# Two-layer image network on one core: x with positions on partitions for the selective scan, projections and LayerNorm moved between images

## The chip, the cores and the metric

The kernel runs on one core of a Trainium2 chip. The metric is the device time of one execution in microseconds. Five engines work in parallel, each through its own instruction queue in order: PE (TensorE), DVE (VectorE), ACT (ScalarE), POOL (GpSimd) and SP (SyncE, which here only issues DMAs).

## The reference

Eight images of 56 x 56 pixels with 192 channels pass two residual layers. Layer 0 (group norm, three gated projections to 576 channels, Toeplitz products along rows and columns) is not touched by the change. Layer 1 is a state-space block on 384 inner channels with 16 states:

```python
xz = gn(x) @ W_in.T
xc, z = split(xz)                       # 384 and 384 channels
xc = silu(depthwise_conv3x3(xc) + conv_b)
# eight orders of the 3136 pixels: rows and columns, there and back, every other line turned round
for k in range(8):
    dt, B, C = split(x_proj_weight[k] @ xs[k])      # 12, 16 and 16 rows
    delta = softplus(dt_projs_weight[k] @ dt + bias)
    h = exp(delta * A) * h + (delta * xs[k]) * B    # step by step along the order
    y[k] = sum_n(h * C) + D * xs[k]
y = layernorm(sum_k(y[k] back in pixel order))
out = x + (y * silu(z)) @ W_out.T
```

## The kernel before

After layer 0 for all images (lines 113 to 370) and a preparation of image 0 (lines 415 to 485), each image has a **scan stage** (488 to 892) and a **LayerNorm stage** (895 to 1217). The LayerNorm stage of image b also prepares image b + 1.

*Scan stage.* The 3136 steps of each of the eight orders are cut into chunks of W = 63, so there are 400 chunks, and three blocks of 128 channels for each: 1200 units per image. A unit is one `tensor_tensor_scan` on DVE over 16 states of 64 elements (`scan`, L740). It reads `da` = exp(delta * A) from ACT (`exps`, L704: 16 instructions for four chunks of one channel block) and `bx` from PSUM (`products`, L725: the products of delta * x with B for all states, as matmuls with a block-diagonal image of B). Before the scan ACT copies the last state of the chunk before into `bx` (`before`, L736). After it POOL multiplies h by the broadcast C (`times_c`, L751), PE turns and sums that over the states into `yps` (`sums`, L848), ACT copies it out (L875), and SP stores y with positions as rows (L760).

What a unit needs is made for a group of up to eight chunks (`Group`), in this order: SP loads x with channels on partitions in the order of the scan (`xs`, L542); PE projects it to the rows of steps, B and C (`project`, L549), ACT copies them out, mirrored where the order runs backwards (`projected`, L562); C goes to DRAM and comes back broadcast over partitions (`to_dram`, `broadcast`, L566 and L573); B is written element by element into a zeroed DRAM image along its diagonal and read back (`diagonal_out`, `diagonal_in`, L650 and L658; ten such images, zeroed once at L395); PE and ACT make delta (`steps`, L580, L589, and one softplus for the group, L593). Then for each pair of chunks POOL multiplies delta by x (`product`, L616), PE turns the product so that positions lie on partitions (`turn`, L625), ACT copies it to `dut` (`turned`, L633), and SP makes a second copy with the halves swapped (`swapped`, L641).

A hand-written table (`plan`) gives every step of a group its place relative to the group's first unit f, and a loop over units writes the order on every engine:

```python
s = f - 11 + 6 * p
at("POOL", s - 1, self.product, p)
at("PE", s, self.turn, p)
at("ACT", s + 1, self.turned, p)
```

The scheduler does not reorder (`tc.manual_schedule()`). `px`, `pd` and `pt` share one PSUM bank (`pmisc`, one buffer). Four `da` buffers are in turn.

*LayerNorm stage.* Seven tiles of eight image rows (448 pixels). For each, four loads of `yk` bring the eight y's of 112 pixels (16 DMAs each, three buffers), and PE turns and adds them into `ysum` (96 transposes a tile, L1092). DVE adds D * x (L1111); mean and variance come from matmuls with a matrix of 1/384 (L1123, L1146); the rest is on DVE and ACT with channels on partitions. Beside it, for the next image: projection (L949), convolution as nine matmuls with diagonal weights for each of three channel blocks (L967), and copies of the result in three orders on DVE and POOL (L991, L993, L1010, L1012), stored as `xo`. This stage has a hand-written order too.

Of the kernel before, what the change touches and what calls it, by code (L numbers as in the profile page):

```python
# [70 lines left out]
SC = 4  # L71
SIZES = (8, 8, 8, 8, 8, 8, 2)
# [16 lines left out]
def conv_kernel(ctx: ExitStack, tc: tile.TileContext, a: dict, out: bass.AP):  # L89
# [18 lines left out]
    gstat = const.tile([CP, B, 2, 2], F32, name="gstat")  # L108

# [274 lines left out]

    xod = [[dram.tile([128, NB, L], F32, name=f"xo{b}_{o}") for o in range(3)] for b in range(B)]
    ytd = [dram.tile([K, L, DI], F32, name=f"yt{b}") for b in range(B)]

    bdd = [dram.tile([2, 64 * 64 * N], F32, name=f"bd{i}") for i in range(NI)]  # L390
    with tc.tile_pool(name="none", bufs=1) as p:
        none = p.tile([128, 64 * N], F32, name="none")
        nc.vector.memset(none, 0.0)
        for t in bdd:
            nc.sync.dma_start(t.rearrange("h (s x) -> (h s) x", s=64), none)  # L395

    def halves(t):

        return t.rearrange("p d (h w) -> p d h w", w=HW)

    for b in range(B):

        def normed(pool, t):

            x1 = pool.tile([CP, 2, T], F32, name="x1")
            nc.sync.dma_start(x1, x1d[b][:, :, t * T : (t + 1) * T])
            xn = pool.tile([CP, 2, T], F32, name="x1n")
            for c in range(2):
                nc.vector.tensor_scalar(
                    xn[:, c], x1[:, c], gstat[:, b, c, 0:1], gstat[:, b, c, 1:2], ALU.subtract, ALU.mult  # L410
                )
            return x1, xn


        if b == 0:
            with ExitStack() as st:
                one = st.enter_context(tc.tile_pool(name="prep1", bufs=1))
                pre = st.enter_context(tc.tile_pool(name="prep", bufs=2))
                pm = st.enter_context(tc.tile_pool(name="pp", bufs=4, space=PSUM))
                win = one.tile([CP, 2, 2 * DI], F32, name="win")  # L420
                nc.sync.dma_start(win, a["W_inT"])
                xp = [one.tile([128, HW + 2, HW + 2], F32, name=f"xp{d}") for d in range(NB)]
                dg = one.tile([128, NB, 9, 128], F32, name="dg")
                for d in range(NB):
                    for edge in (xp[d][:, 0, :], xp[d][:, HW + 1, :], xp[d][:, :, 0], xp[d][:, :, HW + 1]):
                        nc.gpsimd.memset(edge, 0.0)  # L426
                    for j in range(9):
                        nc.vector.tensor_scalar(
                            dg[:, d, j, :], ident, cw[:, d, j : j + 1], None, ALU.mult
                        )  # L430
                for t in range(NT):
                    _, xn = normed(pre, t)
                    for d in range(NB):
                        pp = pm.tile([128, T], F32, name="pp")
                        for c in range(2):
                            nc.tensor.matmul(
                                pp, win[:, c, d * 128 : (d + 1) * 128], xn[:, c], start=(c == 0), stop=(c == 1)
                            )
                        nc.scalar.copy(
                            xp[d][:, 1 + t * RT : 1 + (t + 1) * RT, 1 : HW + 1],  # L440
                            pp.rearrange("p (h w) -> p h w", w=HW),
                        )
                xc = one.tile([128, NB, L], F32, name="xc")
                xcv = xc.rearrange("p d (h w) -> p d h w", w=HW)
                for t in range(NT):
                    for d in range(NB):
                        pc = pm.tile([128, RT, HW], F32, name="pc", tag="pp")
                        for j in range(9):
                            dy, dx = divmod(j, 3)
                            nc.tensor.matmul(  # L450
                                pc,
                                dg[:, d, j, :],
                                xp[d][:, t * RT + dy : t * RT + dy + RT, dx : dx + HW],
                                start=(j == 0),
                                stop=(j == 8),
                            )
                        nc.scalar.activation(
                            xc[:, d, t * T : (t + 1) * T],
                            pc.rearrange("p h w -> p (h w)"),
                            AF.Silu,  # L460
                            bias=cb[:, d : d + 1],
                        )
                    for o in range(2):
                        xo = pre.tile([128, NB, T], F32, name=f"xo{o}")
                        for par in range(2):
                            src = xcv[:, :, t * RT + par : (t + 1) * RT : 2, :]
                            dst = halves(xo)[:, :, par::2, :]
                            if par != o:
                                src = src[:, :, :, ::-1]
                            if o:  # L470
                                nc.gpsimd.tensor_copy(dst, src)
                            else:
                                nc.vector.tensor_copy(dst, src)
                        nc.sync.dma_start(xod[b][o][:, :, t * T : (t + 1) * T], xo)
                xct = xcv.rearrange("p d h w -> p d w h")
                for t in range(NT):
                    xo = pre.tile([128, NB, T], F32, name="xo2", tag="xo0")
                    for par in range(2):
                        src = xct[:, :, t * RT + par : (t + 1) * RT : 2, :]
                        dst = halves(xo)[:, :, par::2, :]  # L480
                        if par:
                            nc.gpsimd.tensor_copy(dst, src[:, :, :, ::-1])
                        else:
                            nc.vector.tensor_copy(dst, src)
                    nc.sync.dma_start(xod[b][2][:, :, t * T : (t + 1) * T], xo)


        with ExitStack() as st:
# [11 lines left out]
            das = [one.tile([128, SC, N, W + 1], F32, name=f"da{i}") for i in range(4)]  # L500
            for t in das:
                nc.gpsimd.memset(t[:, :, :, 0], 0.0)
            dus = [one.tile([128, NB, 2, W + 1], F32, name=f"du{i}") for i in range(2)]
            for t in dus:
                nc.gpsimd.memset(t[:, :, :, W], 0.0)
# [6 lines left out]
            class Group:  # L512


                def __init__(self, k, c0, nch, i):
# [7 lines left out]
                    self.bufs = 1 if self.small else 2  # L523
                    u0 = c0 * W
                    self.m = min(self.n, L - u0)
                    self.p0 = L - u0 - self.m if self.rev else u0
                    self.cb, self.dut, self.bd = [], [], []

                def load(self):
                    if self.c0 == 0:  # L530
                        xpw = pre.tile([128, NB, XR], F32, name="xpw")
                        nc.sync.dma_start(xpw, a["x_proj"][:, :, self.k, :])
                        dtw = pre.tile([R + 1, DI], F32, name="dtw")
                        nc.sync.dma_start(dtw, a["dt_w"][:, self.k, :])
                        weights[self.k] = xpw, dtw
                    n, m = self.n, self.m
                    self.xs = pre.tile([128, NB, n], F32, name="xs", tag="xs" + self.tag, bufs=self.bufs)
                    lo = n - m if self.rev else 0
                    if m < n:
                        z = slice(0, n - m) if self.rev else slice(m, n)  # L540
                        nc.gpsimd.memset(self.xs[:, :, z], 0.0)
                    nc.sync.dma_start(  # L542
                        self.xs[:, :, lo : lo + m], xod[b][self.o][:, :, self.p0 : self.p0 + m]
                    )

                def project(self, d):
                    if d == 0:
                        self.px = pmisc.tile([XR, 512], F32, name="px", tag="misc")
                    nc.tensor.matmul(  # L549
                        self.px[:, : self.n],  # L550
                        weights[self.k][0][:, d],
                        self.xs[:, d],
                        start=(d == 0),
                        stop=(d == NB - 1),
                    )

                def projected(self):
                    self.pxs = pre.tile([XR, self.n], F32, name="pxs", tag="pxs" + self.tag, bufs=self.bufs)
                    src = self.px[:, : self.n]
                    if self.rev:  # L560
                        src = src[:, ::-1]
# [333 lines left out]
        with ExitStack() as st:  # L895
# [293 lines left out]
            for t in range(NT):  # L1189
# [14 lines left out]
                if Z:  # L1204
                    Z.project()
# [86 lines left out]
```

## Time and profile before

| | us |
|---|---|
| median of 3 runs | 30519.63 |
| lowest and highest | 30509.42, 30534.07 |
| profiled execution | 30517.28 |
| its span | 30515.5 |
| PE, DVE, ACT, POOL busy | 28382.8, 23796.3, 22305.0, 22200.9 |
| first scan of image 0, of image 1 | 3671.3, 7055.4 |
| last scan of image 0, of image 7 | 6554.3, 30241.6 |

The profiled execution takes 1.8 us more than its span, which is what lies around it. Busy time is that of one engine; engines work at the same time, so these don't add up. In lines of the costliest groups stand line, engine, operation, output <- inputs with partitions x elements, the count, then busy us, mean ns of one, and the idle time in front with what ended it. A fp32 matmul has two records. Back-to-back instructions of DVE overlap a little: a scan is recorded with 2.26 us, and starts follow each other by 2.177 us at best.

### The profile page before, as it was taken

To read this page: it belongs to the slowest core of one execution; us is meant where nothing else is said; L and a number is where in the kernel's file an instruction comes from. 1 tells how busy PE (TensorE), PEld (TensorE's weight loads), DVE (VectorE), ACT (ScalarE), POOL (GpSimd) and SP (SyncE) were. 2 spreads that over 40 slices of the span, in tenths; PEclk is the share of its full clock that TensorE was granted. 3 is DMA by queue.
4 is the path that set the end of the run, shared out by engine and by line. 5 is a ranking of instruction groups with operands and counts; after the bars stand their busy time and mean duration, and the time that the engine had idled before them with its cause. 6 is when DMAs were issued, how large, how long until landed. Compare 5 with 4: busy or idle time off the path is not lost.

```text
span 30515.5 us, 475124 instructions
## 1 busy us (share of the span) xinstructions
PE 28382.8 (93%) x156976; PEld 16133.2 (53%) x156976; DVE 23796.3 (78%) x13460; ACT 22305.0 (73%) x58955; POOL 22200.9 (73%) x11592
## 2 busy tenths in 40 slices
PE   7999899988999899989999899989999899989998
PEld 5555455554555455554555455545555455545555
DVE  3444399967999499958998599949997699949997
ACT  2233388857898488848898488849887588848886
POOL 0000299957999399948998499939997599939996
PEclk9999999999999899999999999999999999989999
DMA  3222355555555555555555555545555555545555
GB/s 80 64 59 59 81 150 151 149 149 143 151 151 149 140 151 151 149 144 147 151 150 148 143 149 150 152 139 151 152 150 149 143 149 151 151 140 151 149 151 157
DMA packets 5635967, 4229.72 MB, mean 139 GB/s; under 512 B 3712112, under 2 KB 5007920, under 8 KB 5625968
## 3 DMA queue, kind: packets, MB, share of 16 engines
q1 hardware_dynamic: 5600368, 4192.09, 52.5%
q8 instruction: 1265, 20.73, 0.3%
q10 hardware_dynamic: 33152, 7.23, 0.2%
q14 instruction: 1182, 9.68, 0.1%
HBM read 3389.38 MB, written 508.43 MB: 128 GB/s over the span
## 4 chain that ended last, share of the span: by engine, by line
PE 49%; ACT 9%; POOL 5%; DMA 5%; issue 4%; DVE 3%; SPq 2%; ACTq 0%; POOLq 0%; DVEq 0%
PE bx L725 18%; PE yps L848 17%; ACT da L704 5%; POOL hc L751 5%; PE px L549 3%; PE pc L967 3%; PE pd L580 2%; DVE h L740 2%; DMA cbt<-cd 2%; PE pt L625 1%; DMA yt<-yt 1%; PE ysum L1092 1%; ACT L704 1%; ACT L593 1%; PE pp L949 1%
## 5 line engine op out<-in xcount | busy, mean ns | idle before, releaser
L740 DVE TENSOR_TENSOR_SCAN h<-da,bx 128x1024 f32<-128x1024 f32 x9600 | 21374.7, 2273 | 2122.0 <-ACT bx L736 1862.3
L751 POOL TENSOR_TENSOR hc<-h,cbt 128x1008 f32<-128x1008 f32 x9600 | 20552.9, 2167 | 1289.0 <-PE yps L848 584.9
L704 ACT ACTIVATE da<-delta,A_logs 128x252 f32<-128x252 f32 (+1 forms) x39936 | 17030.9, 489 | 76.7 <-DVE h L740 66.2
L725 PE MATMUL bx<-bd,dus 63*128 63x504 f32 x19200 | 10468.4, 633 | 223.2 <-DVE h L740 219.8
L725 PE MATMUL bx<-bd,dut 63*128 63x504 f32 x19200 | 10453.4, 633 | 224.3 <-DVE h L740 222.4
L848 PEld LDWEIGHTS yps<-ident,hc 128*126 128x126 f32 x76800 | 8360.9, 141 | 4045.8 <-issue 2361.8
L848 PE MATMUL yps<-ident,hc 128*126 128x128 f32 x76800 | 9500.1, 277 | 458.4 <-ACT yt L875 423.8
L725 PEld LDWEIGHTS bx<-bd,dut 63*128 63x128 f32 x19200 | 2901.9, 186 | 2616.4 <-DVE h L740 1531.0
L725 PEld LDWEIGHTS bx<-bd,dus 63*128 63x128 f32 x19200 | 2903.3, 186 | 1085.1 <-issue 664.0
L736 ACT COPY bx<-h 128x16 f32<-128x16 f32 x9408 | 1655.5, 176 | 1658.1 <-PE bx L725 1606.4
L426 POOL MEMSET xp<- 128x58 f32 x12 | 1.3, 193 | 3402.0 <-DMA x<-x1d 3401.9
L991 POOL COPY xo<-xp 128x672 f32<-128x672 f32 x98 | 70.5, 749 | 2852.9 <-ACT xp L974 2852.9
L616 POOL TENSOR_TENSOR du<-delta,xs 128x378 f32<-128x378 f32 x1600 | 1588.2, 993 | 174.9 <-ACT delta L593 173.6
L549 PE MATMUL px<-xs,xpw 128*64 128x504 f32 (+1 forms) x2688 | 1237.3, 571 | 215.5 <-DMA xs<-xo 215.5
L875 ACT COPY yt<-yps 126x256 f32<-126x256 f32 x2400 | 862.8, 360 | 719.1 <-PE yps L848 708.3
L580 PE MATMUL pd<-pxs,dtw 13*128 13x504 f32 x2304 | 1299.4, 644 | 68.2 <-ACT dut L633 29.3
L625 PEld LDWEIGHTS pt<-ident,du 128*128 128x128 f32 x4800 | 498.8, 141 | 1252.8 <-issue 565.6
L974 ACT ACTIVATE xp<-pc,conv_b 128x448 f32<-128x448 f32 x147 | 93.4, 636 | 1346.5 <-PE pc L967 1346.4
L967 PE MATMUL pc<-xp,dg 128*128 128x448 f32 x2646 | 1019.6, 538 | 0.0
L1111 DVE SCALAR_TENSOR_TENSOR y<-xc,dsum,ysum 128x224 f32<-128x224 f32 x336 | 125.4, 442 | 1133.6 <-PE ysum L1092 1133.6
L625 PE MATMUL pt<-ident,du 128*128 128x128 f32 x4800 | 880.6, 293 | 45.3 <-POOL du L616 38.4
L549 PEld LDWEIGHTS px<-xs,xpw 128*64 128x64 f32 x2688 | 298.6, 138 | 1116.0 <-issue 873.9
(137 smaller groups left out, 16721.2 us busy)
## 6 DMA issues: line engine op xcount, KB each, us to landing
cbt<-cd SPq DMA_DIRECT2D x1600, 1008.0 KB
bd<-bd SPq DMA_DIRECT2D x3200, 256.0 KB
dus<-dut SPq DMA_DIRECT2D x3200, 96.0 KB
yk<-yt SPq DMA_DIRECT2D x3584, 84.0 KB
yt<-yt SPq DMA_DIRECT2D x9408, 31.5 KB
xs<-xo SPq DMA_DIRECT2D x384, 756.0 KB
xo<-xo SPq DMA_DIRECT2D x168, 672.0 KB
bd<-pxs SPq DMA_DIRECT2D x3200, 3.9 KB
```

Source lines behind the costliest of these rows:

```text
L549: nc.tensor.matmul(self.px[:, : self.n], weights[self.k][0][:, d], self.xs[:, d], start=(d == 0), stop=(d == NB - 1),)
L580: nc.tensor.matmul(self.pd[:, : self.n], weights[self.k][1][:, d * 128 : (d + 1) * 128], self.pxs[0 : R + 1], start=True, stop=True,)
L616: nc.gpsimd.tensor_mul(self.du[:, :, :, :W], self.delta[:, :, part].rearrange("p d (c t) -> p d c t", t=W), xs[:, :, part].rearrange("p d ...
L625: nc.tensor.transpose(self.pt[:, d * 128 : (d + 1) * 128], self.du[:, d].rearrange("p c t -> p (c t)"), ident,)
L704: yield nc.scalar.activation(da[:, : self.nc, n, 1:], src.rearrange("p (c t) -> p c t", t=W), AF.Exp, scale=an[:, G.k, self.d, n : n + 1],)
L725: nc.tensor.matmul(self.bx[:, r, :, 1:], G.dut[p][q ^ r][rows, self.d * 128 : (self.d + 1) * 128], G.bd[p][rows, q, :, :W], start=True, st ...
L736: nc.scalar.copy(self.bx.rearrange("p r n t -> p (r n) t")[:, :, 0], src)
L740: nc.vector.tensor_tensor_scan(self.h.rearrange("p n t -> p (n t)"), das[self.P.buf][:, self.slot].rearrange("p n t -> p (n t)"), self.bx. ...
L751: nc.gpsimd.tensor_tensor(hc, self.h[:, :, 1:], self.G.cb[self.c // 2][:, :, q * W : (q + 1) * W], ALU.mult)
L848: nc.tensor.matmul(yps[:, t // 4 % 2, t // 2 % 2], lhsT=hcs[t // 2][:, n].rearrange("p c t -> p (c t)"), rhs=ident, start=(n == 0), stop=( ...
L875: nc.scalar.copy(y, yps[:, s // 4 % 2])
L967: nc.tensor.matmul(pc, dg[:, d, j, :], xp[:, d, t * RT + dy : t * RT + dy + RT, dx : dx + HW], start=(j == 0), stop=(j == 8),)
```

## The change

*x for the scan.* x is stored in DRAM with one pixel's 384 channels as a row (`xtd`), in three orders. A pair of chunks is loaded with positions on partitions (`inputs`, four buffers `xts`). delta alone is turned by PE, and DVE multiplies the turned delta in PSUM by x into `dut`. POOL's `product`, ACT's `turned` and the loads of `xs` are gone. For orders that run backwards nothing is mirrored ahead: delta is kept in pixel order, and the exponentials, the product with C and the places of stores are read backwards instead.

*Projections.* The rows of steps, B and C for all eight orders are made in the stage between images, with two directions of one order in one matmul of 128 rows (`rows`), and stored in `pxd` by DMAs of ACT's queue. The scan stage loads steps (`dt`), C (`cd`) and B's diagonals from `pxd`. There are twenty zeroed images for the diagonals (backward orders have their own), written ahead of layer 0's weights instead of after layer 0.

*Stage between images.* One class for preparation and LayerNorm, run for b = -1 to 7, in an order found by the scheduler instead of written by hand. y is stored with the directions of one order side by side, so a load of four rows has two DMAs of 3072-byte rows and four of 6144-byte rows (`load_y`, six buffers). POOL and DVE add the eight y's and D * x with positions on partitions; mean and variance of a pixel come from `bn_stats`; the scaling is one ACT instruction for 112 pixels, and only then PE turns the sum (12 transposes a tile). The convolution of channel blocks 0 and 2 runs on DVE, that of block 1 on PE. PE turns the convolved x (12 transposes a tile), and SP stores it in the orders; the mirrored lines of two orders are copied from DRAM to DRAM (`mirror`).

*Scan stage, smaller edits.* Five `da` buffers (`NR`); the softplus of a small group in three instructions; other places of the first large group's steps.

The core of the diff:

```diff
 class Group:
     def load(self):
-        self.xs = pre.tile([128, NB, n], F32, name="xs", ...)
-        nc.sync.dma_start(self.xs[...], xod[b][self.o][:, :, self.p0 : self.p0 + m])
+        self.dt = pre.tile([R + 1, self.n], F32, name="dt", tag="dt" + self.tag, bufs=1)
+        nc.sync.dma_start(*self.part(self.dt, 0, R + 1, 0, self.m, self.n))
+        self.cd = cdp.tile([GC // 2, N, 2 * W], F32, name="cd")
+        for p in range(self.npr):
+            nc.sync.dma_start(*self.part(self.cd[p], 48, N, p * 2 * W, e, 2 * W))
-    def project(self, d): ...
-    def projected(self): ...
-    def to_dram(self): ...
+    def inputs(self, p):
+        xt = self.xt[p] = xts[(self.i // 2 + p) % 4]
+        nc.sync.dma_start(xt, lines_of(xtd[b][self.o], at, (W, 2), (1, W + 1)))
+        ...
-    def product(self, p):
-        nc.gpsimd.tensor_mul(self.du[:, :, :, :W], self.delta[...], xs[...])
     def turn(self, p):
         nc.tensor.transpose(
             self.pt[:, d * 128 : (d + 1) * 128],
-            self.du[:, d].rearrange("p c t -> p (c t)"),
+            self.delta[:, d, first : first + 2].rearrange("p c t -> p (c t)"),
             ident)
-    def turned(self, p):
-        nc.scalar.copy(dut, self.pt[:, :DI])
+    def product(self, p):
+        nc.vector.tensor_mul(dut, self.pt[:, :DI], self.xt[p])
     def diagonal_out(self, p):
-        nc.sync.dma_start(to, self.pxs[32 : 32 + N, u : u + W]...)
+        nc.sync.dma_start(to, pxd[b][self.place, 32 : 32 + N][:, u : u + e]...)
     def plan(self, at):
-        at("POOL", s - 1, self.product, p)
+        at("SP", x if soon and p == 0 else s - 6, self.inputs, p)
         at("PE", s, self.turn, p)
-        at("ACT", s + 1, self.turned, p)
+        at("DVE", s + 1, self.product, p)
 ...
 class Unit:
     def times_c(self, hc):
+        if self.G.rev:
+            q, h = 1 - q, h[:, :, ::-1]
         nc.gpsimd.tensor_tensor(hc, h, self.G.cb[...], ALU.mult)
 ...
 class Next:      # the next image
     def conv(self):
+        for j in range(9):
+            for d in range(NB):
+                if d == 1:
+                    nc.tensor.matmul(acc, dg[:, j], src, start=(j == 0), stop=(j == 8))
+                elif j:
+                    nc.vector.scalar_tensor_tensor(acc, src, w, acc, ALU.mult, ALU.add)
+                else:
+                    nc.vector.tensor_scalar(acc, src, w, None, ALU.mult)
+    def rows(self, g):
+        nc.tensor.matmul(ps, pxw[:, d, g], x[:, t * RT : (t + 1) * RT], ...)
+        nc.scalar.activation(dst, src, AF.Identity, bias=pxb)       # twice, every other line
+        nc.scalar.dma_start(to[:, t * T : (t + 1) * T], px)
 ...
 class Tile:      # LayerNorm of this image
+    def pairs(self, i):
+        nc.gpsimd.tensor_tensor(xt, xt, dsb, ALU.mult)
+        nc.gpsimd.tensor_tensor(yk[:, 0:4], yk[:, 0:4], yc, ALU.add)
+    def total(self, i):
+        nc.vector.tensor_add(yk[:, 0:2], yk[:, 0:2], yk[:, 2:4])
+        nc.vector.tensor_add(yk[:, 0], yk[:, 0], yk[:, 1])
+        nc.vector.tensor_add(ys, yk[:, 0], xt)
+        nc.vector.bn_stats(self.st[:, i], ys)
+        nc.vector.bn_aggr(self.mv[:, i], self.st[:, i : i + 1])
-    def centre(self): ...
-    def scale(self): ...
```

## The prediction

> **What bounds the kernel now.** I read the busy table first, then the costliest groups, then stretches of the span, then the chain of waits.
>
> ```profile
> PE 28382.8 (93%) x156976; PEld 16133.2 (53%) x156976; DVE 23796.3 (78%) x13460; ACT 22305.0 (73%) x58955; POOL 22200.9 (73%) x11592
> ...
> L740 DVE TENSOR_TENSOR_SCAN h<-da,bx 128x1024 f32<-128x1024 f32 x9600 | 21374.7, 2273 | 2122.0 <-ACT bx L736 1862.3
> L751 POOL TENSOR_TENSOR hc<-h,cbt 128x1008 f32<-128x1008 f32 x9600 | 20552.9, 2167 | 1289.0 <-PE yps L848 584.9
> ...
> L616 POOL TENSOR_TENSOR du<-delta,xs 128x378 f32<-128x378 f32 x1600 | 1588.2, 993 | 174.9 <-ACT delta L593 173.6
> L549 PE MATMUL px<-xs,xpw 128*64 128x504 f32 (+1 forms) x2688 | 1237.3, 571 | 215.5 <-DMA xs<-xo 215.5
> ```
>
> All four engines are near full, so shares alone decide nothing. The busy time by stretch (start and end, length; PE, PEld, DVE, ACT, POOL; granted clock; DMA share; GB/s) separates the stages:
>
> ```profile
> 3405.00:3671.00 266.00, 202.04 (x505) 95.60 (x505) 33.41 (x62) 41.23 (x71) 24.71 (x43) 0.84 0.31 95
> 3671.00:6557.00 2886.00, 2772.20 (x15613) 1555.95 (x15613) 2671.98 (x1202) 2580.05 (x7031) 2746.97 (x1405) 0.99 0.58 149
> 6557.00:7055.00 498.00, 386.99 (x1445) 217.22 (x1445) 129.41 (x209) 82.73 (x121) 26.55 (x44) 0.86 0.49 142
> ...
> 30244.00:30515.00 271.00, 198.75 (x943) 126.33 (x941) 96.45 (x148) 42.94 (x51) 2.15 (x1) 0.84 0.62 183
> ```
>
> Layer 0 takes 3405 us, the preparation of image 0 takes 266; then come eight scan stages of 2886, seven LayerNorm stages of 498 between them, and a tail of 271. In a scan stage the chain of waits in order of time (start, us, what) shows the beat:
>
> ```profile
> 8056.16 1.04 PE bx L725 x4
> 8057.20 1.83 PE px L549 x4
> 8059.04 1.04 PE bx L725 x4
> 8060.08 1.90 PE yps L848 x16
> ...
> 8068.00 0.48 PE pt L625 x3
> ...
> 8072.47 1.04 PE pd L580 x2
> ```
>
> PE runs without a gap: per unit (one scan) 1.045 us of bx and half of 1.90 of yps; per six units 0.48 of pt; per 24 units three pd of 1.04 and three px of 1.04. That is 1.045 + 0.95 + 0.08 + 0.13 + 0.13 = 2.335, or 2800 for 1200 units. **PE sets the scan stage**, at 97% of 2886. POOL is next (2747 busy), DVE third. Who waited for whom in the second scan stage agrees (us, times, longest):
>
> ```profile
> DVE h L740 <- ACT bx L736: 241.1, 304, 53.5
> ...
> ACT bx L736 <- PE bx L725: 201.9, 268, 2.3
> ```
>
> DVE waits for ACT's small copy, and ACT for PE.
>
> [...] the zero images written at 3399 to 3416 reached 362.
>
> **The change, part by part.**
>
> *Scan stage, PE.* px goes: 2.335 - 0.13 = 2.205 a unit, 2646 a stage.
>
> *Scan stage, POOL.* du goes (993 ns per six units, 0.165). What stays starts every 2.12 to 2.17: at most 2600. Reading h backwards in half of the directions I cost at nothing: the layout copies on POOL (L991), one of two mirrored, take 742 to 753 ns throughout.
>
> *Scan stage, ACT.* The copies of pt (91 us) and px (33) go: 2580 - 124 = 2456. The splitting of the small softplus into three adds 3. A fifth da buffer lets the exponentials run further ahead.
>
> *Scan stage, DVE.* 200 products of 384 elements, PSUM by SBUF. Nearest row: y<-y,p, 448 elements, 617 ns, one every 0.53 us in a row; less 64 elements at 1.04 ns (the slope from 448 to the 896 of L307, 1084 ns), 0.47 us. Scans start every 2.177 us at best: 1200 x 2.177 + 200 x 0.47 = 2706. **DVE becomes the longest engine.** Bounds for one product: 0.40 (384 elements alone) to 0.56 (not overlapped).
>
> *Stalls.* Today 86 us a stage lie above PE's 2800, mostly after each softplus, where ACT loads two tables and catches up. With less on ACT I keep 60: 2766, so -118 against 2884, eight times: **-944**. Bounds: 2726 (-1264 in all) and no gain.
>
> *New waits in the scan.* The product stands in DVE's queue behind one scan and ahead of the next, so all scans queue behind its wait, and bx and PE behind them. It waits for PE's turn, which follows the bx of two units ahead: 1.04 + 0.48 after the scan two before it ended, some 2.8 us early; and for xt, issued seven units (16 us) before. Cover for both; if it went, each us would cost 1600 us.
>
> *SP.* It issues for 1495 of 2800 us. One or two xt loads per pair and three more cd loads a group, less one xs: about 300 of 0.45 to 0.6, +150. B's diagonals move from SBUF to DRAM as source; their 4-byte packets hold 8% of the DMA engines today. Hidden while DMA stays near 58%.
>
> *LayerNorm stage, 501 from last scan to first.* Three parts: 10 until PSUM and SBUF are free, 438 of tiles, 53 until the first scan. PE now, per tile of seven: three convolutions of 6.93, 96 transposes 9.8, means 4.8, three projections of 4.6 = 49.2. After: one convolution 6.9, turning x 1.9, B/C/steps four times three matmuls of 0.75 = 9, turn back 1.2, projections 14: 33, or 231 a stage. DVE after: 18 convolution steps of 0.6, sums of four rows 2.5 each, the rest 5: 26 a tile, 183. POOL: 28 times 1.0 and 3.15 (linear in L616 and L751): 116. [...] DVE and POOL take up to 299 together. DMA: y 38.5 MB, x and its copies 19, projections 6.4, input and output 7: 71 MB, at the 213 to 264 GB/s of today's tail 270 to 330. Three limits lie at 260 to 330; I take 320 for the tiles. The lead loses the xs load, px and the second group's front: 30. Sum 360, -141, seven times: **-987**. Bounds 330 to 478.
>
> *Preparation.* 266 becomes PE 157 at today's 0.76 busy share, 206, plus the shorter lead, less what overlaps: 216, **-50** (0 to -80). *Tail.* 48 MB instead of 46, in packets of 3 and 6 KB instead of 1.5: **-55** (0 to -80). *Start.* Twenty zero images of 512 KB stand on SP and in DMA before layer 0's weights, not ten before the preparation: 10.5 MB at 362 GB/s, **+29**.
>
> **Sum:** 29 - 50 - 944 - 987 - 55 = -2007, from the profiled execution's 30517.3 (span 30515.5): 28510. The median of the three runs, 30519.6, is 2 us away.
>
> **Rivals.** (1) *The scan stage keeps its beat* because the softplus stalls, not PE, set it. Against: the chain is PE gapless for 24 units. For: 20 us of ACT stand on the chain at each softplus. 30517 + 29 - 50 - 987 - 55 = 29450. (2) *The LayerNorm stage turns into a DMA[...] wait* and only the lead is gained: 7 x -23, no tail: 29390. For: three limits are close, and SP's queue is in order, y loads behind stores of x. Against: the tail moves 183 GB/s already. (3) *Slower: the product convoys.* If each product waits for PE's turn, DVE and PE wait in turns. It decides from 2007/1600 = 1.25 us a product; at a whole scan, 2.18, it gives 30517 - 2007 + 3488 = 32000. Against: the 2.8 us of lead. (4) *Nothing of the kind happens* since each removed piece was cover: within 0.2%, which is about what a measurement of this kernel can tell from no change.
>
> **How the numbers follow.** My sum 0.60, rival 1 0.16, rival 2 0.17, rival 3 0.06, rival 4 0.01. Faster is the first three, 0.93. The range goes from 27800 (scan at 2726, LayerNorm 330, prep and tail -80 each, rounded down) to 29450, which takes in rivals 1 and 2.
>
> **What would show it.** Right: scan pitch near 2.30, DVE busiest there with the scan waiting under 100 us a stage for ACT; du, px and dut gone; from last scan to first near 360; layer 0 ending 30 later. Wrong: DVE waiting for pt or xt at the product; a pitch of 2.4; POOL's adds or DVE's convolution steps stretched well over the prices above; y loads late with DMA below 200 GB/s.

## Result and profile after

The changed kernel takes **34587.5 us** (median of 4 runs, 34568.5 to 34608.9) against 30525.1 for the kernel before beside it: a ratio of 1.1332 [1.1312, 1.1351], 13% slower. The forecast was 28510, with 27800 to 29450 as range. The profiled execution has a span of 34607.1 us.

First the page of the kernel after: its busy table, the chain of waits that ended last by engine and by line, and the groups that answer to those shown of before.

```profile
PE 27995.1 (81%) x148912; PEld 16042.3 (46%) x148912; DVE 24974.8 (72%) x16084; ACT 22009.1 (64%) x58050; POOL 21635.3 (63%) x10384
...
DMA 33%; PE 29%; SPq 14%; DVE 7%; POOL 7%; issue 6%; ACT 4%; POOLq 0%; ACTq 0%; DVEq 0%
DMA cbt<-cd 13%; PE bx L985 9%; PE yps L1109 8%; POOL hc L1013 6%; DMA bd<-bd 6%; DMA yr<-yt 6%; DVE h L1000 6%; SPq L908 4%; PE pp L255 3%; ACT da L964 3%; SPq L1023 2%; DMA bd<-pxd 2%; SPq L581 2%; SPq L575 2%; PE po L310 1%
...
L1013 POOL TENSOR_TENSOR hc<-h,cbt 128x1008 f32<-128x1008 f32 x9600 | 20418.9, 2164 | 4761.0 <-DMA cbt<-cd 3865.9
L1000 DVE TENSOR_TENSOR_SCAN h<-da,bx 128x1024 f32<-128x1024 f32 x9600 | 21173.0, 2267 | 2771.5 <-POOL hc L1013 1969.7
...
L606 POOL TENSOR_TENSOR yr<-yr,yc 112x1536 f32<-112x1536 f32 x224 | 771.7, 3445 | 4137.6 <-DMA yc<-yt 2788.7
...
L883 DVE TENSOR_TENSOR dut<-pt,xt 128x384 f32<-128x384 f32 x1600 | 856.8, 535 | 911.4 <-PE pt L875 230.4
```

Every engine's share of the span has fallen. The same line of before, by engine, reads

```profile
PE 49%; ACT 9%; POOL 5%; DMA 5%; issue 4%; DVE 3%; SPq 2%; ACTq 0%; POOLq 0%; DVEq 0%
```

The chain has moved from PE to DMA and SP's queue. The durations on DVE and POOL are those of before: a scan 2267 ns (2273 before), an hc, the product of h with C, 2164 (2167 before). What is new stands in the last column: POOL idles 3866 us ahead of hc for `cbt`, the broadcast of C, which the change hardly touches, and 2789 us ahead of the sums of y for `yc`, one of the loads of y.

The stretches (start and end, length; busy PE, PEld, DVE, ACT, POOL; granted clock; DMA share; GB/s) are the second scan stage, the first LayerNorm stage and the tail:

```profile
7580.00:10721.00 3141.00, 2798.02 (x15293) 1623.89 (x15292) 2729.09 (x1397) 2485.81 (x6786) 2564.45 (x1215) 0.94 0.58 138
6841.00:7580.00 739.00, 315.16 (x757) 140.73 (x757) 221.45 (x342) 140.24 (x253) 135.03 (x82) 0.68 0.33 104
33982.00:34607.00 625.00, 114.64 (x274) 52.94 (x272) 122.73 (x190) 64.01 (x93) 137.87 (x57) 0.57 0.25 79
```

A scan stage grew from 2883 to 3134 us on average instead of falling to 2766, a LayerNorm stretch (last scan to first) from 501 to 744 instead of falling to 360, the tail from 274 to 627. In the scan stage DMA has the share that it had before, 0.58. In the others it has 0.33 and 0.25, and no engine is busy half the time: something waits, and neither the mean share of DMA nor a busy engine shows what for.

Who waited for whom (us, times, longest), in the scan stage from 7600 to 10700 and then in the LayerNorm stage:

```profile
POOL hc L1013 <- DMA cbt<-cd: 477.7, 130, 11.2
...
DVE h L1000 <- POOL hc L1013: 239.9, 102, 7.9
```

```profile
POOL yr L606 <- DMA yc<-yt: 393.4, 21, 30.6
DVE yr L613 <- POOL yr L606: 315.5, 24, 17.2
```

POOL waits for a transfer, and the scan for POOL, since its h buffers are not released.

**Theory T1.** The trace records when each DMA packet (one row of a transfer) starts and ends, and these records show what the share hides. In the tail exactly two packets are in flight for 67% of the time, and 14 or more for 7%. The packets of 3072 bytes (`yr`) take 125 ns at the median, two at a time. For the loads concerned the change writes the outermost dimension of the address as a count of 2: two image lines (a `load_y` takes 112 pixels, which is two lines and not the four said above), or two chunks. The trace also holds the updates that the landing of a DMA makes to its semaphore: 3 for each of these loads (`yr`, `xty` and the pair's `xt`), 5 for a mirror copy, whose outermost count is 4, 15 for a load of 28 rows (`yc`) or of 56 (`yk` in the kernel before), 16 for the 128 rows of `cbt`. `yr`, with its 3, has two packets in flight for 57% of the tail and more than two for 4%. So my estimate is one DMA engine fewer than updates up to 15: two for a count of 2, the same two each time, and 14 for 28 or 56 rows; for the 128 rows of `cbt`, all 16 that the profile counts. The trace has no engine numbers, so it can't show which two, but the tail agrees in how many: its 6272 `yr` packets of 139 ns (mean) and 3136 `xty` packets of 71 ns come to 1094 us, 547 on each of two engines, in 625. It also agrees that they are the same two from load to load: for 68% of the tail two loads of `yr` are issued and, by their semaphores' updates, not yet landed, and for 65% of that time still only two packets are in flight. In the scan stage the same two would carry `xt` on top of their share of everything else, and every transfer over 16 engines would end with them. In the second scan stage `cbt` looks like that: two of its packets are in flight for 13% of the time and 14 for 10%, where before has 16 for 12% and two for 1%.

### The profile page after: what moved, and what is told of

It is laid out like the page before. It is cut to its first block, busy times and chain, and to the rows that moved or that the text cites. A ratio compares the mean times of both kernels' runs of the same rounds, so it can differ in the third digit from the quotient of the medians.

```text
span 34607.1 us, 460315 instructions
## 1 busy us (share of the span) xinstructions
PE 27995.1 (81%) x148912; PEld 16042.3 (46%) x148912; DVE 24974.8 (72%) x16084; ACT 22009.1 (64%) x58050; POOL 21635.3 (63%) x10384
## 4 chain that ended last, share of the span: by engine, by line
DMA 33%; PE 29%; SPq 14%; DVE 7%; POOL 7%; issue 6%; ACT 4%; POOLq 0%; ACTq 0%; DVEq 0%
DMA cbt<-cd 13%; PE bx L985 9%; PE yps L1109 8%; POOL hc L1013 6%; DMA bd<-bd 6%; DMA yr<-yt 6%; DVE h L1000 6%; SPq L908 4%; PE pp L255 3%; ACT da L964 3%; SPq L1023 2%; DMA bd<-pxd 2%; SPq L581 2%; SPq L575 2%; PE po L310 1%
## 5 line engine op out<-in xcount | busy, mean ns | idle before, releaser
L1013 POOL TENSOR_TENSOR hc<-h,cbt 128x1008 f32<-128x1008 f32 x9600 | 20418.9, 2164 | 4761.0 <-DMA cbt<-cd 3865.9
L1000 DVE TENSOR_TENSOR_SCAN h<-da,bx 128x1024 f32<-128x1024 f32 x9600 | 21173.0, 2267 | 2771.5 <-POOL hc L1013 1969.7
L985 PE MATMUL bx<-bd,dus 63*128 63x504 f32 x19200 | 10813.4, 653 | 1811.2 <-DVE h L1000 1403.8
L985 PE MATMUL bx<-bd,dut 63*128 63x504 f32 x19200 | 10771.3, 651 | 816.7 <-DVE h L1000 806.8
L1109 PEld LDWEIGHTS yps<-ident,hc 128*126 128x126 f32 x76800 | 8975.2, 148 | 3889.4 <-issue 2635.3
L1109 PE MATMUL yps<-ident,hc 128*126 128x128 f32 x76800 | 10151.6, 289 | 32.4 <-ACT yt L1136 17.8
L606 POOL TENSOR_TENSOR yr<-yr,yc 112x1536 f32<-112x1536 f32 x224 | 771.7, 3445 | 4137.6 <-DMA yc<-yt 2788.7
L883 DVE TENSOR_TENSOR dut<-pt,xt 128x384 f32<-128x384 f32 x1600 | 856.8, 535 | 911.4 <-PE pt L875 230.4
L836 PE MATMUL pd<-dt,dtw 13*128 13x504 f32 x2304 | 1311.6, 649 | 175.9 <-DMA dt<-pxd 113.1
L875 PEld LDWEIGHTS pt<-ident,delta 128*128 128x128 f32 x4800 | 502.4, 142 | 1240.8 <-issue 995.1
L875 PE MATMUL pt<-ident,delta 128*128 128x128 f32 x4800 | 884.9, 294 | 34.9 <-ACT delta L851 27.9
L836 PEld LDWEIGHTS pd<-dt,dtw 13*128 13x128 f32 x2304 | 344.9, 187 | 1058.1 <-issue 733.4
```

The source lines that it names most:

```text
L836: nc.tensor.matmul(self.pd[:, : self.n], weights[self.k][:, d * 128 : (d + 1) * 128], self.dt, start=True, stop=True,)
L875: nc.tensor.transpose(self.pt[:, d * 128 : (d + 1) * 128], self.delta[:, d, first : first + 2].rearrange("p c t -> p (c t)"), ident,)
L883: nc.vector.tensor_mul(dut, self.pt[:, :DI], self.xt[p])
L985: nc.tensor.matmul(self.bx[:, r, :, 1:], G.dut[p][q ^ r ^ int(G.rev)][rows, self.d * 128 : (self.d + 1) * 128], G.bd[p][rows, q, :, :W], s ...
L1000: nc.vector.tensor_tensor_scan(self.h.rearrange("p n t -> p (n t)"), das[self.P.buf][:, self.slot].rearrange("p n t -> p (n t)"), self.bx. ...
L1013: nc.gpsimd.tensor_tensor(hc, h, self.G.cb[self.c // 2][:, :, q * W : (q + 1) * W], ALU.mult)
```

## Experiments

**One part each undone: where the loads' outermost count is 2.** In the scan stage (`scan16`):

```diff
-nc.sync.dma_start(xt, lines_of(lines, at, (W, 2), (1, W + 1)))
+for c in range(2):
+    nc.sync.dma_start(xt[64 * c : 64 * c + 64], lines_of(lines, at + c * W, (1, W + 1)))
```

> Edit: in the scan stage the 128 x rows of a pair come by two loads of 64 rows each, not by one load whose outermost step counts 2. Same bytes, same rows, 200 more DMA issues per scan stage. Theory T1 (a load whose outermost dimension counts 2 is carried by two of the 16 DMA engines, which then are late with their share of the cbt loads that hc waits for): the pitch of the scans in a scan stage falls from 2.61 us to about 2.30, the wait of hc for cbt from some 480 us a stage to under 100; the time falls by 8 x 350 to about 31800 us (31200 to 32400); the stretch from last scan to first scan stays near 743 us and the tail near 627. Rival A (the 4-byte DRAM-sourced diagonals, 1.5 us to issue, block SP's queue and the DMA engines): pitch stays at 2.55 or more, total within 400 us of 34590, since SP's work even grows by 200 issues. Rival B (the product on DVE convoys with PE): pitch stays at 2.6.

Measured: 31762.7 us, 1.0407 [1.0391, 1.0422] of before. The pitch (mean time from one scan to the next within a stage) is 2.316 to 2.324 us, stages 2777 to 2787, the LayerNorm stretches 737 to 740, the tail 630. A scan stage of `scan16`; then the group of hc in the kernel after (its second stage), and the groups of the scan and of hc in the second stage of `scan16`:

```profile
3706.00:6485.00 2779.00, 2656.30 (x15269) 1514.33 (x15265) 2710.28 (x1397) 2475.37 (x6793) 2579.16 (x1214) 0.99 0.61 156
```

```profile
L1013 POOL TENSOR_TENSOR hc<-h,cbt 128x1008 f32<-128x1008 f32 x1199 | 2550.4, 2164 | 598.0 <-DMA cbt<-cd 508.7 <-PE yps L1109 51.1 <-DVE h L1000 27.2
```

```profile
L1001 DVE TENSOR_TENSOR_SCAN h<-da,bx 128x1024 f32<-128x1024 f32 x1199 | 2637.6, 2264 | 70.0 <-ACT bx L997 59.3 <-POOL hc L1014 10.6
L1014 POOL TENSOR_TENSOR hc<-h,cbt 128x1008 f32<-128x1008 f32 x1198 | 2564.4, 2164 | 217.7 <-DVE h L1001 136.7 <-DMA cbt<-cd 50.9 <-PE bx L986 2.4
```

With the same bytes and 160 more DMAs a stage, the wait for `cbt` falls from 509 us to 51, and POOL now waits mostly for the scan. By the packet records the last of a `cbt`'s 128 packets lands 4.9 us after its issue (median), where it took 9.8 in the kernel after. Exactly two packets of any kind were in flight for 16% of that stage, now for 3%; exactly two packets of `cbt`, whatever else was under way, for 13%, now for 1%. Rivals A and B are out: SP's 4-byte diagonals and the product are unchanged, and the pitch is right. The late loads act in a second place too: in the second stage of the kernel after SP's in-order queue waits 396 us for `xt` to land before it can issue other DMAs, in `scan16` under 3 (for the way of this wait see T2). How much of the stage's loss goes each way was not separated. **The scan stage as forecast was there, under these loads.**

In the LayerNorm stage (`ln14`): loads of 56 rows, and the mirror copy with 56 outermost in place of 4, all read forward. So the kernel leaves out the mirroring of lines, as do `both14`, `pxq`, `lag1`, `pxlate` and `noy` below.

```diff
-nc.sync.dma_start(yr[:, 2 * o : 2 * o + 2]..., two(ytd[b][o], odd != o))
+for i in range(2):
+    nc.sync.dma_start(yr[i * HW : (i + 1) * HW, 2 * o : 2 * o + 2]..., line(ytd[b][o], odd != o, i))
```

> Edit: in the LayerNorm stage the y and x lines come in loads of 56 consecutive rows each (two where there was one with an outermost count of 2), and the mirror copy has the 56 positions outermost, not the 4 lines. The mirroring of lines is left out of these loads and of that copy (they read forward); bytes and packet sizes are the same, SP has more issues. Theory T1: these loads spread over 14 DMA engines; the stretch from last to first scan falls from 743 us to between 350 and 420, the tail from 627 to about 250 to 300, the scan pitch stays at 2.61; the time falls by 7 x 350 + 350 to about 31800 us (31300 to 32400). Rival C (the LayerNorm stage is held [...] by the order of work on the in-order queues): the stretch stays above 650 us and the tail above 550, total above 33900.

Measured: 32631.3 us, 1.0691 [1.0676, 1.0707]. Stretches 516 to 522 us, tail 289, pitch 2.60 to 2.63; the first scan of image 0 starts at 3653 in place of 3697. The direction is T1's and rival C is out, but over a third of the gain that I expected between last and first scan is missing, and the time lies above the expected range. Count and reading direction change together in this edit, but the direction costs nothing by itself in the tail of the kernel after: a `yr` packet takes 138 ns on average in the loads that read forward and 139 in the mirrored ones.

> Both edits together (the mirroring of lines in the LayerNorm stage's loads and copy is left out). Theory T1: the two gains add up: about 29000 us (28500 to 29800), near the 28510 that was forecast for the change; what is left above it is the price of terms that the forecast missed otherwise. Rivals A to C: no less than 33500.

Measured: 29800.8 us, 0.9764 [0.9747, 0.978]. The gains add up: 2825 and 1956 apart, 4787 together. The 800 us above T1's 29000, at the upper end of what was expected, lie in the LayerNorm stretches (513 to 518). Stretches of this kernel: a LayerNorm stage and the tail.

```profile
6437.00:6953.00 516.00, 320.22 (x781) 144.70 (x781) 249.14 (x342) 135.22 (x242) 140.68 (x83) 0.76 0.52 147
...
29524.00:29805.00 281.00, 118.27 (x299) 55.90 (x300) 161.21 (x189) 64.07 (x93) 138.19 (x58) 0.67 0.65 176
```

In the tail 14 packets or more are in flight 58% of the time now. Exactly 14, the number estimated under T1 for loads of 56 rows, is the commonest, with 32%.

**The suspected cause put into the kernel before.** A spare load of 128 rows of 1536 bytes per pair, which nothing reads, in two forms:

```diff
 rows = bass.AP(x.tensor, x.offset + u * DI, ...
+    [[W * DI, 2], [DI, W + 1], [1, DI]])   # bk2
+    [[DI, 128], [1, DI]])                  # bk16
+nc.sync.dma_start(spare[(self.i // 2 + p) % 4], rows)
```

> The kernel before, with one spare load added per pair of units: 128 rows of 1536 bytes from xo into a tile that nothing reads, the outermost dimension of the load counting 2 (two blocks of 64 rows). 196 KB a pair, about 4.8 us of engine time if spread over 16 engines at the 65 to 75 ns that such packets take, 1.6 GB in all. Theory T1 (two DMA engines carry all of it, and loads that are spread over 16 wait for their share on those two): the scan pitch rises from 2.404 to between 2.55 and 2.7 us, hc waits for cbt for over 300 us a stage, the time rises by 5 to 10% to 32000 to 33500 us. Rival (more bytes, more issues on SP, whatever the form): within 1.5% of before, like its twin.

> The kernel before with the same spare load per pair, same bytes and same packets, but as 128 consecutive rows in one dimension. Theory T1: spread over 16 engines, the time stays within 1.5% of before (30500 to 31000 us), the pitch within 0.03 us of 2.404. Rival (bytes or issues): slower by the same 5% or more as its twin.

Measured: `bk2` 32654.3 us, 1.0696 [1.0665, 1.0727]; `bk16` 30512.2, 0.9997 [0.9987, 1.0007]. A scan stage of each, `bk2` first, and then `bk2`'s waits there:

```profile
7317.00:10469.00 3152.00, 2867.53 (x15586) 1612.64 (x15586) 2652.46 (x1199) 2590.03 (x7030) 2733.67 (x1403) 0.95 0.62 149
```

```profile
7062.00:9939.00 2877.00, 2763.17 (x15587) 1548.04 (x15588) 2668.20 (x1199) 2578.00 (x7027) 2744.53 (x1403) 1.00 0.63 163
```

```profile
DVE h L748 <- POOL hc L759: 417.1, 159, 9.1
POOL hc L759 <- DMA cbt<-cd: 391.1, 107, 9.1
```

One more transfer of 196 KB costs nothing at a DMA share of 0.63, and 7% at 0.62. The pitch of `bk2`, 2.62 to 2.63, and the landing of its `cbt`, 10.1 us after issue (5.3 in `bk16`, 5.0 in before), are close to those of the changed kernel. The form of one load is enough to bring a scan stage of before to the length that it has in the kernel after (3147 us on average, against 3134). Both forms are one issue on the same queue, so the count of issues is out too. (Two figures in the first of these expectations are off, without bearing on its forecast: 128 packets of 65 to 75 ns are 8 to 10 us of engine time, so 4 to 5 us on each of two engines and 0.6 on each of sixteen, and the 1600 loads carry 0.31 GB.)

**The rest of the LayerNorm stage.** In the version with both edits y loads still came late. SP's own waits there from 6640 to 6870 (us, times, longest):

```profile
SPq L576 <- DMA pxd<-px: 44.8, 5, 14.9
SPq L583 <- DMA pxd<-px: 23.6, 4, 13.1
SPq L588 <- DMA pxd<-px: 17.6, 3, 12.4
```

Loads of y wait for stores of B, C and steps (`pxd`), with which they share no data. By the trace of the kernel after, the DMAs of SP and ACT take the same eight semaphores, 101 to 108, in turn as completion counters, and 19343 of these 27670 DMAs wait for their own semaphore at the issue, that is until its last user has landed. A `pxd` store that ACT will issue only once PE has made its rows holds one of the eight (theory T2). By the instructions' times the buffers of y had been free for 42 to 103 us when their loads were issued, and POOL started its add mostly 1 to 5 us after the last issue.

> The version with both edits, in which the stretch from last to first scan still takes 515 us where 360 was forecast; here the stores of B, C and steps (pxd) are issued from the queue of GpSimd and not of ScalarE. Theory T2 (each DMA of SP and ACT takes one of eight completion counters in turn and waits until the one eight before has landed; SP's y loads therefore wait for a pxd store that ACT has not yet issued, 12 to 15 us in each of seven steps): the stretch falls from 515 to about 420 us (400 to 450), the time to about 29150 us. Rival D (the step of 53 us is the chain of one tile through PE, ACT and DVE, or DMA's rate): the stretch stays within 15 us of 515. Rival E: the store now stands in POOL's queue before the adds of y and the wait moves there: the stretch stays or grows.

> The version with both edits, with LAG = 1 in place of 4: the y part of the LayerNorm stage follows the x part by one step, not by four, so that the four steps of some 25 us in which no y is loaded are gone, and B, C and steps of the next image stand alone at the end. Theory F (the stage is a sum of a part without y loads and seven y steps, not the longest of three limits): the stretch falls from 515 to about 450 us (430 to 480) and the time to about 29350 us. Rival: the y steps take longer as the x work falls into them, the end without y grows, and the stretch stays within 20 us of 515.

Measured: `pxq` (`nc.gpsimd.dma_start` for the store) 29751.6 us, 0.9745 [0.9717, 0.9773], stretches 503 to 511; `lag1` 29843.2, 0.9775 [0.9747, 0.9803], stretches 516 to 523. Theory F falls: in `lag1` starting y earlier gains nothing. In `pxq` the y loads do run ahead (from the eighth unit of 112 pixels on, the last issue is 14 to 60 us before POOL's add), and rival E has it: POOL's longest wait, from 6560 to 6900, is

```profile
POOL pxd L515 <- ACT px L513: 224.1, 17, 35.3
```

T2 was not refuted by that, only moved. So the store was put where nothing waits behind it, one step later and after that step's y loads (`pxlate`); and, in another kernel, most y loads were left out (`noy`).

```diff
-nc.scalar.dma_start(to[:, t * T : (t + 1) * T], px)
+held.append((to[:, t * T : (t + 1) * T], px))   # issued on SP after the next step's load_y calls
```

> The version with both edits; the stores of B, C and steps of a tile are issued one step later, from SP's queue and behind that step's y loads (six px buffers in place of three), so that no y load stands behind a completion counter of a store that is still to be issued, and POOL's queue holds no store. Theory T2 (those counters set the 53 us step of the LayerNorm stage): the stretch from last to first scan falls from 515 to about 430 us, the time to about 29250. Theory G (the step is a chain through the in-order engines: adds on POOL, sums on DVE, root on ACT, scales on DVE, scaling on ACT, turning on PE, gate on ACT, product on DVE, projection on PE): y is loaded early, and the stretch stays above 490 us.

> The version with both edits, with the y and x lines of only the first six of an image's 28 units loaded; the other 22 units use those six sets of tiles again, so their 48 MB are left out. Theory G (chain through the engines): the stretch from last to first scan stays above 470 us. Theory T2 or a limit in the DMA engines: it falls below 420 us; PE alone has 320 us of work there at the granted clock, DVE 250, POOL 140. The tail, which has no other image's work beside it, falls from 281 to below 250.

Measured: `pxlate` 29354.4 us, 0.9616 [0.9597, 0.9636], stretches 443 to 451; `noy` 29169.6, 0.9556 [0.9537, 0.9575], stretches 428 to 430, tail 257. A LayerNorm stage of `pxlate`, then of `noy`:

```profile
6442.00:6890.00 448.00, 307.12 (x777) 140.15 (x777) 284.69 (x343) 135.02 (x248) 152.37 (x83) 0.80 0.61 171
```

```profile
6428.00:6857.00 429.00, 299.52 (x778) 135.19 (x778) 267.40 (x342) 133.45 (x244) 153.53 (x83) 0.82 0.34 98
```

The counters cost 68 us of 515 a stage: most of T2's 85. The edit also gives `px` six buffers for three, but these were not the wait: in a LayerNorm stage of `both14` the copies into `px` wait for PE alone. Most of what is left, 447, is not y's transfers: with four fifths of them gone (34 MB an image) it is 429. That lies between the two forecasts for `noy`, so neither theory as written accounts for it, and the tail, 257, misses its 250. `noy` kept the store on ACT, and SP waits 19 us for it in the first of its LayerNorm stages, so its 429 is not a floor.

**A version with the whole computation.** `best` splits, beside `xt`, only the loads that read forward; `best2` also has the later store.

> A version with all of the computation: the scan edit, and in the LayerNorm stage only the loads that read forward are split into 56-row loads; those that read mirrored keep an outermost count of 2. Theory T1: [...] the stretch from last to first scan falls from 743 to about 450 to 550 us and the tail from 627 to about 400; the time is about 29900 us (29300 to 30800), which is 2% below the kernel before. Rivals: as for the two single edits, above 33500.

> All of the computation: x in two loads of 64 rows in the scan stage, forward lines in 56-row loads in the LayerNorm stage, and the later store of B, C and steps. Theory T2: the stretch falls from 578 us by up to 60, the time from 30453 to about 30100 (29900 to 30400). Theory G, with the mirrored loads on two DMA engines setting the pace: 30350 to 30500.

Measured: `best` 30453.1 us, 0.9978 [0.9969, 0.9987], stretches 574 to 581, tail 446; `best2` 30299.7, 0.9927 [0.9911, 0.9944], stretches 559 to 563, scan stages 2779 to 2787. Both times lie in the upper part of what was expected of T1 and T2; `best`'s stretches and tail are longer than expected. What `best2` keeps and `pxlate` does not are the mirrored loads with a count of 2 and the mirror copy with a count of 4; with them the LayerNorm stage takes 560, without them 447. But **`best2` takes 0.7% less than the kernel before and 12% less than the changed one**. A mirrored load of 56 rows in one dimension, with a negative outermost step, was not tried.

## Why the prediction was wrong

The terms of the sum, from first scan to end, and where each was recovered. Measured sums are over all stages of a profiled execution; the last column is what the edits to the loads alone took back.

| term | forecast | after | miss | taken back by loads |
|---|---|---|---|---|
| first scan of image 0 at | 3650 | 3697 | +47 | -44 (`ln14`) |
| eight scan stages | 22128 | 25075 | +2947 | -2820 (`scan16`) |
| seven LayerNorm stretches | 2520 | 5208 | +2688 | -1572 (`ln14`) |
| tail | 216 | 627 | +411 | -338 (`ln14`) |
| sum | 28514 | 34607 | +6093 | -4774 |

*The step that failed* is the treatment of DMA as one resource with a mean share: in the scan stage "Hidden while DMA stays near 58%", in the LayerNorm stage "71 MB, at the 213 to 264 GB/s of today's tail 270 to 330". The share did stay at 0.58. But I priced `xt` by its count on SP and the y loads by their bytes, and did not look at how each is cut over the DMA engines. By the dimensions in the kernel after, the loads of `two` (the lines of y and x in `load_y`) and of the pair's x have an outermost count of 2. The rate that I took from before came from loads of 28 and 56 rows. In the kernel after DMA moved 104 GB/s in the LayerNorm stretch and 79 in the tail, which is one of the prediction's own signs of being wrong ("y loads late with DMA below 200 GB/s"). 4774 of the 6093 us came back when the form of these transfers was mended.

*Scan stage, PE, DVE, ACT and POOL: right.* With the loads mended the pitch is 2.316 to 2.324, where "near 2.30" was to show it, DVE is the busiest engine (2710 of 2779 us), and the scan waits 59 us for ACT's small copy. The forecast stage of 2766 is measured at 2782, so rival 1, that the beat stays, is out. The product takes 532 ns at the median, and puts 0.45 us between scans (2.626 us from scan to scan at the median, less 2.177), where I took 0.47. Reading h backwards costs nothing (hc takes 2142 to 2220 ns in all orders of the second stage).

*Rival 3, the product convoys: wrong mechanism, right sign.* It was to be seen in DVE waiting for pt or xt at the product; in the second scan stage of the kernel after that is 1.6 and 9.0 us. I gave 0.06 to slower because the only way to it that I worked out lay on the engines, and none on the queues of DMA; that one of the rivals ran the right way is luck.

*LayerNorm stage.* Rival 2 named the right kind of cause, a wait for DMA, but bounded it at nothing lost, since it again took bytes over the old rate. Beyond the loads, the seven stretches of `both14` sum to 3605, 1085 above the forecast: 475 of it are the shared counters (`pxlate` has 3130), which I had not looked for at all though I had counted SP's queue; 610 remain, 87 a stage, and stay open. The engines' terms were too small there. In `pxlate`, less what its stretch holds of the next scan stage (22, 6 and 9 us): PE 231 against 285 (projections of B, C and steps are 12 matmuls of 1.17 us a tile, where I took 0.75), DVE 183 against 278 (a convolution step takes 0.97 us on average, where I took 0.6), POOL 116 against 143. The convolution steps on DVE were long where an add of POOL lay beside them: the 84 of 112 steps with no add of POOL beside them take 680 ns at the median and 689 at most, the eleven that lie almost wholly beside one 3.7 us, about an add's length (3.4). Above 680 ns each, the steps hold DVE 32 us a stage. And taking the longest of three limits supposes that steps which hand a tile from engine to engine overlap fully. Which of these holds the 447 us was not tried.

*Preparation and start: right to 3 us* once the mirror copy is spread (3653 against 3650), and part by part: layer 0 ends 28 us later in `ln14`, where I took 29. The 44 us come back with the mirror copy as it was, too, when the store is put later (`best2`, 3657): in the preparation of the kernel after SP waits 101 us for `pxd` stores, by the counters of T2.

## What to carry to other kernels

Price a DMA by its engines as well as by its bytes: read off the outermost count of its address (in `bk2` a count of 2 cost 7%, in `bk16` 128 rows cost nothing) before you believe a rate, and compare a load's form with that of the row that its rate comes from. Two overloaded DMA engines, as T1 has them, did not show in a mean share (0.58 in the scan stage, before and after); what showed here was a wait for another, unchanged, evenly spread transfer that landed late (`cbt`, 509 us a stage), and a number of packets in flight that stood at two (16% of that stage, 67% of the tail). When an in-order queue waits for a transfer with which it shares no data, as SP's did for `pxd` for up to 15 us at a time, look for the counter, not for the buffer.

## What the runs showed that I had not expected

- One added load of 196 KB per pair, in the same queue, with the same packets, costs 7% in one form and nothing measurable in the other.
- Transfers that are spread evenly pay for it: `cbt` lands 9.8 us after issue in place of 4.9, with unchanged bytes.
- A store queued on ACT delays loads on SP by up to 15 us at a time through the shared completion counters; putting it later gains 68 us of a 515 us stage.
- A convolution step that takes 680 ns on DVE takes 3.7 us where it lies almost wholly beside an add on POOL.
